# State-space scans in a fused decoder kernel: from 128 channels times one state to 8 channels times 16 states on the partitions

## The chip, the cores and the metric

The kernel runs on one core of a Trainium2 chip, in fp32 throughout the part that is discussed. The metric is the device time of one execution in microseconds. A core has five engines with instruction queues of their own: TensorE (PE, with its weight loads as PEld), VectorE (DVE), ScalarE (ACT), GpSimd (POOL) and SyncE (SP), which here issues all the DMAs.

## The reference, cut to what matters

A decoder of four layers runs on 4 sequences of 256 tokens with 256 features. Each layer has an attention part, a second mixing part and a feed-forward part; every part ends with a residual sum and a layer norm. In layers 0 and 1 the second mixing part is a state-space scan over the context `ctx_1024` (4 x 256 x 128), gated by the stream `x`, with 256 inner channels and 16 states per channel:

```python
x = einsum('ed,bld->bel', in_proj_w, hidden_states)      # 256 channels
u = silu(depthwise causal conv of 4 taps over x + conv_b)
x_dbl = einsum('ke,bel->bkl', x_proj_w, u)               # 8 + 16 + 16 rows
dt_lo, Bm, Cm = x_dbl[:, :8], x_dbl[:, 8:24], x_dbl[:, 24:]
delta = softplus(einsum('er,brl->bel', dt_proj_w, dt_lo) + dt_proj_b)
A = -exp(A_log)                                          # 256 x 16
def step(state, (d_t, B_t, C_t, u_t)):                   # state: b x 256 x 16
    state = state * exp(d_t[..., None] * A) + (d_t * u_t)[..., None] * B_t[:, None, :]
    return state, einsum('ben,bn->be', state, C_t)
y = (outputs of the steps + D * u) * silu(z)             # z is the stream x
```

Only the gate needs `x`. The scan itself depends on the context alone, so it can run beside other work.

## The kernel before

Features or channels lie on the 128 partitions in two chunks (DC = 2); a row of a tile runs over tokens. The program is written with the Tile framework: pools hand out buffers, semaphores are derived from the tiles' use, and the framework's scheduler puts the instructions of each engine into a fixed order when the program is built. On the chip every engine takes its queue in that order.

The class `Scans` holds both state-space passes. `begin(pre)` starts the generator `_steps` and `beside(n)` moves it on by n steps, so that the attention code can place scan steps between its own. `upto(b)` moves it on until sequence b is done, and `gate_pair` then gates that sequence, turns it back and adds it to the stream.

Pass one (`l0x`) runs beside the multi-query attention `run_mqa`: 32 pieces, n = 0 to 31, eight per sequence, each of four heads by 128 rows. A piece has scores, maxima (`nm`) and exponentials, transposes, sums (`o`) and an output product into the bank `acc`; the projections of query pairs (`queries`, with the rotation on DVE: `ropet`, `qT`) run four pieces ahead. In each piece the loop calls `K.scans.beside(2)`, and `gate_pair` is called for sequences 0, 1 and 2 at n = 10, 18 and 26 and for sequence 3 after the loop.

Pass two (`l1x`) is begun inside `run_thought`, a chain of four dependent iterations on 4 tokens followed by a gating of the whole stream; that function ends with `K.scans.beside(24)`. The rest runs beside the grouped attention `run_gqa`, one generator step per tile and then one per attention step. Its `gate_pair` calls are due after each sequence's attention.

Within `_steps` (lines 443 to 532) a prologue makes `u` (the convolution is folded into four matmuls with `taps`), writes the B and C rows to DRAM (`bcd`), and makes `delta` and `du = delta * u`, which stay in SBUF with 128 channels on the partitions. Then one generator step handles one state n of one sequence b for both chunks, 2 x 256 columns per partition:

- a DMA brings the B and C row of this state, spread over all partitions (`bc`, 256 KB);
- ACT makes two exponentials of 255 columns into `dA`, whose first column stays zero, so that the scan starts afresh at each chunk;
- DVE multiplies (`s = du * B`), scans over 512 columns (line 521) and multiplies by C;
- two steps later PE adds `s` to a PSUM bank by a product with the 128x128 identity (`ssmps`, fp32). After 16 states DVE adds the skip term and writes the result into `u`.

That makes 64 generator steps per pass, 16 for each sequence. `wk` gives four buffers for `bc` and for `s`, `dA` has three, and there is one PSUM bank.

Of the kernel before, what the change touches and what calls it, by code (L numbers as in the profile page):

```python
# [19 lines left out]
F32 = mybir.dt.float32  # L20
# [5 lines left out]
AF = mybir.ActivationFunctionType  # L26
# [4 lines left out]
ADD, SUB, MUL, MAX, MIN = ALU.add, ALU.subtract, ALU.mult, ALU.max, ALU.min  # L31

P = 128
B, L, D = 4, 256, 256
NT = B * L // P
DC = D // P
# [170 lines left out]
def again(ap, n):  # L207

    return ap.unsqueeze(1).to_broadcast([ap.shape[0], n, ap.shape[1]])
# [23 lines left out]
def run_mqa(K, w, more):  # L233
    nc, tc = K.nc, K.tc
    with ExitStack() as ctx:
        one = ctx.enter_context(tc.tile_pool(name="mqa1", bufs=1))
        wk = ctx.enter_context(tc.tile_pool(name="mqa2", bufs=2))
# [119 lines left out]
        N = 8 * B  # L357
# [3 lines left out]
        y = K.scans.y  # L361
# [6 lines left out]
        for n in range(N):  # L368
            shares(n)
            if n + 1 < N:  # L370
                scores(n + 1)
            if n + 4 < N:
                queries(n + 4)
            if n in (2, 3, 4, 5):
                rest.pop(0)()
            if n == 6:
                ready = ready_thought(K, more()) if K.fused(0) else iter(())
            if n > 9:
                next(ready, None)
            K.scans.beside(2)  # L380
            turn(n)
            if n:
                output(n - 1)
            sums(n)
            if n % 8 == 2 and n > 8 and K.fused(0):
                gate_pair(K, wk, y, n // 8 - 1)
        output(N - 1)
        if K.fused(0):
            gate_pair(K, wk, y, B - 1)
# [3 lines left out]

SSM_COLS = 19


class Scans:
    def __init__(self, K, ctx):  # L400
        tc = K.tc
        self.K = K
        self.one = ctx.enter_context(tc.tile_pool(name="ssm1", bufs=1))
        self.wk = ctx.enter_context(tc.tile_pool(name="ssm2", bufs=4))
        self.ps = ctx.enter_context(tc.tile_pool(name="ssmp", bufs=1, space=PSUM))
        self.dram = ctx.enter_context(tc.tile_pool(name="ssmd", bufs=2, space=bass.MemoryType.DRAM))

        self.dA = [self.one.tile([P, DC, L], F32, name=f"dA{k}") for k in range(3)]
        for t in self.dA:
            K.nc.gpsimd.memset(t[:, :, 0:1], 0.0)  # L410
        self.w = {}
        self.left = iter(())
        self.done = 0

    def load(self, pre):
        K = self.K
        self.w[pre] = {
            "in": K.load(self.one, f"{pre}_in", [P, D]),
            "xp": K.load(self.one, f"{pre}_xp", [P, DC, 40], "(c p) n -> p c n", p=P),
            "dt": K.load(self.one, f"{pre}_dt", [8, D]),  # L420
            "cols": K.load(self.one, f"{pre}_cols", [P, DC, SSM_COLS], "(c p) n -> p c n", p=P),
        }

    def bank(self):
        return self.ps.tile([P, 512], F32, name="ssmps", tag="ps")

    def begin(self, pre):

# [12 lines left out]
            next(self.left, None)  # L441

    def _steps(self, pre):
        K, nc, w, wk = self.K, self.K.nc, self.w[pre], self.wk
        cols = w["cols"]
        N = B * L
        u = self.one.tile([P, DC, N], F32, name="u", bufs=2)
        delta = self.one.tile([P, DC, N], F32, name="delta")
        du = self.one.tile([P, DC, N], F32, name="du")


        taps = []
        for j in range(4):
            t = wk.tile([P, D], F32, name="tap", tag="bc", padded_shape=[P, 2 * L])
            nc.sync.dma_start(out=t, in_=K.A[f"{pre}_cw"][:, j * D : (j + 1) * D].to_broadcast([P, D]))
            K.ptt(t, t, w["in"], MUL)
            taps.append(t)
        for h in range(2):
            for c in range(DC):
                ps = self.bank()  # L460
                for j in range(4):
                    K.mm(ps, taps[j][:, c * P : (c + 1) * P], K.ctxp[:, 2 * h : 2 * h + 2, j : j + L], j == 0, j == 3)
                K.act(u[:, c, 512 * h : 512 * h + 512], ps, AF.Identity, bias=cols[:, c, 0:1])
        K.act(u, u, AF.Silu)
        negA = self.one.tile([P, DC, 16], F32, name="negA")
        K.act(negA, cols[:, :, 2:18], AF.Exp)
        K.ts(negA, negA, -1.0, None, MUL)
        bc = self.dram.tile([2, 16, N], F32, name="bcd")
        for h in range(2):
            s = slice(512 * h, 512 * h + 512)  # L470
            xd = wk.tile([P, 512], F32, name="xd", tag="s")
            ps = self.bank()
            for c in range(DC):
                K.mm(ps[0:40, :], w["xp"][:, c, :], u[:, c, s], c == 0, c == DC - 1)
            nc.scalar.copy(xd[0:40, :], ps[0:40, :])
            for k in range(2):
                nc.sync.dma_start(out=bc[k, :, s], in_=xd[8 + 16 * k : 24 + 16 * k, :])
            for c in range(DC):
                ps = self.bank()
                K.mm(ps, w["dt"][:, c * P : (c + 1) * P], xd[0:8, :])  # L480

                K.ts(delta[:, c, s], ps, cols[:, c, 1:2], None, ADD)
                K.act(du[:, c, s], ps, AF.Abs, bias=cols[:, c, 1:2])
        K.act(du, du, AF.Exp, scale=-1.0)
        K.act(du, du, AF.Ln, bias=K.eps[1.0])
        for c in range(DC):
            K.stt(delta[:, c, :], delta[:, c, :], 0.0, du[:, c, :], MAX, ADD)
            K.tt(du[:, c, :], delta[:, c, :], u[:, c, :], MUL)

        turn = 0  # L490
        self.y = u

        late = []
        bank = {}

        def add(b, n, s):
            if n == 0:
                bank[b] = self.bank()
            y = bank[b]
            K.mm(y, K.ident, s.rearrange("p c l -> p (c l)"), n == 0, n == 15)  # L500
            if n == 15:
                for c in range(DC):
                    v = u[:, c, b * L : (b + 1) * L]
                    K.stt(v, v, cols[:, c, 18:19], y[:, c * L : (c + 1) * L], MUL, ADD)
                self.done += 1

        for b in range(B):
            lo = b * L
            for n in range(16):
                yield  # L510
                if len(late) > 1:
                    add(*late.pop(0))
                t = wk.tile([P, 2, L], F32, name="bc", tag="bc")
                nc.sync.dma_start(out=t, in_=bc[:, n, lo : lo + L].unsqueeze(0).to_broadcast([P, 2, L]))
                dA = self.dA[turn % 3]
                turn += 1
                for c in range(DC):
                    K.act(dA[:, c, 1:L], delta[:, c, lo + 1 : lo + L], AF.Exp, scale=negA[:, c, n : n + 1])
                s = wk.tile([P, DC, L], F32, name="s")
                K.tt(s, du[:, :, lo : lo + L], again(t[:, 0, :], DC), MUL)  # L520
                nc.vector.tensor_tensor_scan(  # L521
                    out=s.rearrange("p c l -> p (c l)"),
                    data0=dA.rearrange("p c l -> p (c l)"),
                    data1=s.rearrange("p c l -> p (c l)"),
                    initial=0.0,
                    op0=MUL,
                    op1=ADD,
                )
                K.tt(s, s, again(t[:, 1, :], DC), MUL)
                late.append((b, n, s))  # L530
        for t in late:
            add(*t)


def gate_pair(K, pool, y, b):

    K.scans.upto(b)
    gate = pool.tile([P, DC, L], F32, name="gate")

    K.act(gate, K.x[:, 2 * b : 2 * b + 2, :], AF.Silu)  # L540
    K.ptt(gate, gate, y[:, :, b * L : (b + 1) * L], MUL)
    for t in range(2):
        ps = K.tp.tile([P, 512], F32, name="ps", tag="tp")
        for c in range(DC):
            K.nc.tensor.transpose(ps[:, c * P : (c + 1) * P], gate[:, c, t * P : (t + 1) * P], K.ident)
        K.add_out(2 * b + t, ps[:, 0:D])
# [1782 lines left out]
def _layout(v):  # L2329
# [7 lines left out]

    a["l0a_wq"], a["l0a_wkv"], a["l0a_wout"] = v["L0_attn_Wq"], v["L0_attn_Wkv"], v["L0_attn_Wout"]
    a["l0a_rope"] = _rope_halves()

    for pre, s in (("L0_xattn_", "l0x_"), ("L1_xattn_", "l1x_")):
        g = lambda n, pre=pre: v[pre + n]
        a[s + "in"], a[s + "xp"], a[s + "dt"] = g("in_proj_w").T, g("x_proj_w").T, g("dt_proj_w").T
        a[s + "cw"] = g("conv_w").reshape(D, 4).T.reshape(1, 4 * D)
        a[s + "cols"] = np.concatenate(
            [g("conv_b")[:, None], g("dt_proj_b")[:, None], g("A_log"), g("D")[:, None]], 1
        )

    f = "L0_ffn_"
    for n in ("agg", "d1", "d2", "bc", "gate"):  # L2350
# [106 lines left out]
```

## Time and profile before

| | |
|---|---|
| time, median of 3 runs | 2405.0 us (2401.42 to 2425.04) |
| the profiled execution's own time | 2413.25 us |
| its span in the profile | 2411.4 us |
| busy PE, PEld | 2225.9 us (92%), 1514.3 us (63%) |
| busy DVE, ACT, POOL | 1461.5 us (61%), 788.5 us (33%), 259.7 us (11%) |
| mean granted TensorE clock | 0.948 of full speed |
| bytes moved by DMA | 139.50 MB |
| reads of the B and C rows (`bc<-bcd`) | 128 DMAs of 256.0 KB, 4.6 us from issue to landing |
| scans, line 521 | 128 of 128x512, 1214 ns each |
| first and last scan of pass one, of pass two | 87.7 and 354.7 us; 423.4 and 711.8 us |

Busy times are unions over an engine's instructions. A duration in a list of groups is that of one instruction from start to end; neighbours on one engine overlap somewhat, so the pitch on the timeline is shorter. "<-" after an idle time names what ended it. A released engine tells only of its own wait: idle time of an engine that isn't needed costs nothing.

### The profile page before, as it was taken

The page shows a single profiled execution, that of the slowest core. Times are in us where ns is not written, and L with a number is a line of the kernel's source. Part 1 is how long each engine was busy: PE and PEld are TensorE (multiplying, and loading weights), DVE is VectorE, ACT ScalarE, POOL GpSimd, SP SyncE. Part 2 cuts the span into 40 slices and gives each one's busy share as a digit, 9 for nine tenths or more (in the row PEclk, how much of TensorE's full clock was granted, in tenths as well). Part 3 has the DMA queues.
Part 4 walks back from the last instruction along what each step waited for, and adds up shares of the span by engine and source line. Part 5 has one row for each costly group of instructions (what it writes and reads, how often), then busy time and mean ns, then how long its engine had stood idle before and what let it go on. Part 6 is the DMA issues. An engine that isn't in the chain of part 4 may idle for free. (4 is left out here: it accounts for less than half of the span.)

```text
span 2411.4 us, 28602 instructions
## 1 busy us (share of the span) xinstructions
PE 2225.9 (92%) x10504; PEld 1514.3 (63%) x10504; DVE 1461.5 (61%) x3178; ACT 788.5 (33%) x1763; POOL 259.7 (11%) x419
## 2 busy tenths in 40 slices
PE   7889998589996999899999999999999988899998
PEld 4466664235434655546888888888876545477676
DVE  4899983898975211290355454444555668686366
ACT  4667674333441111162111111111112233243443
POOL 0000011220010322200001100011110001300001
PEclk9999999687986999999999999999997898999999
DMA  6222221232213544220132111120200011100000
GB/s 204 63 60 59 58 53 37 49 81 50 50 34 103 168 128 128 86 77 14 46 100 84 64 46 47 50 71 32 65 1 22 1 59 60 42 1 1 1 1 18
DMA packets 133747, 139.50 MB, mean 58 GB/s; under 512 B 13892, under 2 KB 121766, under 8 KB 131944
## 3 DMA queue, kind: packets, MB, share of 16 engines
q1 hardware_dynamic: 133608, 137.68, 19.9%
q8 instruction: 83, 1.36, 0.2%
q14 instruction: 56, 0.46, 0.1%
HBM read 134.79 MB, written 2.85 MB: 57 GB/s over the span
## 5 line engine op out<-in xcount | busy, mean ns | idle before, releaser
L133 PE MATMUL ps<-xw,xcT 128*128 128x256 f32 (+1 forms) x2304 | 518.9, 382 | 0.3 <-ACT YT L127 0.3
L133 PEld LDWEIGHTS ps<-xw,xcT 128*128 128x128 f32 x2304 | 430.8, 190 | 64.0 <-issue 1.9
L112 DVE TENSOR_TENSOR xp<-ps,xb 128x256 f32<-128x256 f32 x96 | 40.4, 421 | 229.5 <-PE ps L133 229.4
L133 PE MATMUL sc<-kT,qT 32*128 32x256 f32 (+2 forms) x768 | 168.1, 413 | 10.3 <-DVE qn L130 9.7
L133 PE MATMUL ssmps<-s,idz 128*128 128x512 f32 x256 | 147.9, 688 | 23.3 <-DVE s L112 22.4
L127 ACT ACTIVATE dA<-delta,negA 128x255 f32<-128x255 f32 x256 | 118.1, 501 | 136.2 <-DVE s L521 134.7
L521 DVE TENSOR_TENSOR_SCAN s<-dA,s 128x512 f32<-128x512 f32 x128 | 154.0, 1214 | 2.6
L133 PEld LDWEIGHTS sc<-kT,qT 32*128 32x128 f32 (+1 forms) x768 | 106.6, 204 | 74.1 <-issue 44.2
L112 DVE TENSOR_TENSOR hT<-u,a 128x512 f32<-128x512 f32 x48 | 33.1, 691 | 186.3 <-PE u L133 186.3
L127 ACT ACTIVATE sq<-xp 128x1024 f32<-128x1024 f32 x24 | 25.4, 1057 | 314.4 <-DVE xp L112 314.3
L170 POOL TENSOR_SCALAR rstd<-mv 128x2 f32<-128x2 f32 x48 | 11.6, 243 | 944.4 <-DVE mv L162 925.3
L130 DVE TENSOR_REDUCE qn<-sc 128x2 f32<-128x480 f32 (+1 forms) x192 | 87.0, 504 | 40.5 <-PE sc L133 39.6
L127 ACT ACTIVATE e<-sT 128x512 f32<-128x512 f32 x128 | 70.9, 590 | 108.1 <-PE sT L133 106.0
L133 PE MATMUL sT<-q,kT 32*128 32x256 f32 (+1 forms) x384 | 102.1, 506 | 3.9 <-ACT e L127 3.7
L1489 DVE TENSOR_TENSOR_SCAN dec<-xT,idz 128x256 f32<-128x256 f32 (+1 forms) x192 | 89.7, 535 | 22.1 <-DMA xT<-ad 22.1
L127 ACT ACTIVATE a<-g 128x512 f32<-128x512 f32 x48 | 28.7, 599 | 206.7 <-PE g L133 206.7
L133 PEld LDWEIGHTS ssmps<-s,idz 128*128 128x128 f32 x256 | 47.6, 209 | 75.0 <-DVE s L112 42.7
L133 PE MATMUL g<-xT,wj 128*128 128x512 f32 x192 | 92.1, 603 | 0.7 <-ACT rows L101 0.7
L133 PE MATMUL u<-xT,wj 128*128 128x512 f32 x192 | 91.2, 597 | 0.0
L133 PEld LDWEIGHTS y<-wj,hT 128*128 128x128 f32 x384 | 72.9, 190 | 26.6 <-issue 18.2
L133 PE MATMUL ps<-xT,wi 128*128 128x512 f32 x192 | 85.9, 604 | 3.9 <-ACT xin L127 3.9
L112 DVE TENSOR_TENSOR s<-du,bc 128x512 f32<-128x512 f32 x128 | 87.3, 691 | 3.4 <-PE ssmps L133 3.2
(504 smaller groups left out, 4087.8 us busy)
## 6 DMA issues: line engine op xcount, KB each, us to landing
bc<-bcd SPq DMA_DIRECT2D x128, 256.0 KB, 4.6
xw<-in_l2a_xw_dram SPq DMA_DIRECT2D x24, 768.0 KB, 4.9
xT<-ad SPq DMA_DIRECT2D x12, 1024.0 KB, 4.7
wj<-in_l1f_gate_dram SPq DMA_DIRECT2D x48, 128.0 KB, 2.7
wj<-in_l1f_up_dram SPq DMA_DIRECT2D x48, 128.0 KB, 3.1
wj<-in_l1f_down_dram SPq DMA_DIRECT2D x48, 128.0 KB, 3.1
sel<-cwd SPq DMA_DIRECT2D x32, 192.0 KB, 3.1
sel<-cwd SPq DMA_DIRECT2D x32, 128.0 KB, 3.5
```

The source lines that it names most:

```text
L112: self.nc.vector.tensor_tensor(out=out, in0=a, in1=b, op=op)
L127: self.nc.scalar.activation(out, in_, func, **kw)
L130: self.nc.vector.tensor_reduce(out=out, in_=in_, axis=AX.X, op=op, **kw)
L133: self.nc.tensor.matmul(out, lhsT=lhsT, rhs=rhs, start=start, stop=stop)
L170: self.nc.gpsimd.tensor_scalar(out=out, in0=in_, scalar1=add, scalar2=None, op0=ADD)
L521: nc.vector.tensor_tensor_scan(out=s.rearrange("p c l -> p (c l)"), data0=dA.rearrange("p c l -> p (c l)"), data1=s.rearrange("p c l -> p ...
L1489: nc.vector.tensor_tensor_scan(out=dec[:, k, h, :], data0=ap[:, h, at(bb, k, j) : at(bb, k, 2)], data1=K.idz[:, 0 : (2 - j) * P], initial=0.0,
```

## The change

The scan's layout is turned. A partition now holds one of 8 channels times one of 16 states, and a step takes two groups of 8 channels (g = 0, 1) and two sequences: 2 x 512 columns per partition. A pass has two halves (of two sequences each), two chunks c and eight steps k, 32 steps in all. Each step passes two yields, so that there are still 64 of them.

- `delta` and `du` are no longer read in place: both are written to DRAM (`ddd`, two writes of 1 MB), and each step reads back 8 channels, each spread over 16 partitions, by four DMAs of 256 KB on SP.
- The B and C rows are read once per half into `bct` (16 DMAs of 16 rows), in place of 32 reads of 256 KB.
- ACT makes two exponentials of 2 x 255 columns per step, DVE one multiply, one scan and one multiply over 1024 columns.
- The sum over the 16 states becomes two products per step with a 128x32 pattern `ssm_pick`, which writes a band of 32 PSUM partitions; four steps make a band.
- Pools: one ring `piece` of four buffers of 8 KB per partition takes the place of `bc`, `s`, `delta`, `du`, the taps and `xd`; `dA` has two buffers of 1024 columns.
- Pacing: `run_mqa` moves the generator by 2 and 3 steps in turn, and gates sequences 0, 1 and 2 at n = 17, 19 and 27. The input layout gains `ssm_pick` and an `A_log` in the new order.

```diff
-            K.scans.beside(2)
+            K.scans.beside(2 + n % 2)
...
-            if n % 8 == 2 and n > 8 and K.fused(0):
-                gate_pair(K, wk, y, n // 8 - 1)
+            if n in (17, 19, 27) and K.fused(0):
+                gate_pair(K, wk, y, (17, 19, 27).index(n))
...
-        self.dA = [self.one.tile([P, DC, L], F32, name=f"dA{k}") for k in range(3)]
+        self.dA = [self.one.tile([P, 2, 2, L], F32, name=f"dA{k}") for k in range(2)]
...
+        self.pick = K.load(self.one, "ssm_pick", [P, 4, 32], "p (k n) -> p k n", k=4)
...
+    def piece(self, shape):
+        n = int(np.prod(shape))
+        t = self.wk.tile([P, 4 * 512], F32, name="piece", tag="piece")[:, 0:n]
...
+        dd = self.dram.tile([D, 2, N], F32, name="ddd")
+        pair = [self.piece((2, N)) for _ in range(DC)]
+        xd = self.piece((2, 512))
...
         for c in range(DC):
-            K.stt(delta[:, c, :], delta[:, c, :], 0.0, du[:, c, :], MAX, ADD)
-            K.tt(du[:, c, :], delta[:, c, :], u[:, c, :], MUL)
+            K.act(pair[c][:, 1, :], pair[c][:, 1, :], AF.Exp, scale=-1.0)
+        for c in range(DC):
+            K.act(pair[c][:, 1, :], pair[c][:, 1, :], AF.Ln, bias=K.eps[1.0])
+        for c in range(DC):
+            delta, du = pair[c][:, 0, :], pair[c][:, 1, :]
+            K.stt(delta, delta, 0.0, du, MAX, ADD)
+            K.tt(du, delta, u[:, c, :], MUL)
+            nc.sync.dma_start(out=dd[c * P : (c + 1) * P], in_=pair[c])
...
-            K.mm(y, K.ident, s.rearrange("p c l -> p (c l)"), n == 0, n == 15)
+            for g in range(2):
+                band = 2 * (k // 4) + g
+                K.mm(y[32 * band : 32 * band + 32, :], self.pick[:, k % 4, :], s[:, g, :], k % 4 == 0, k % 4 == 3)
...
-        for b in range(B):
-            lo = b * L
-            for n in range(16):
-                yield
-                if len(late) > 1:
-                    add(*late.pop(0))
-                t = wk.tile([P, 2, L], F32, name="bc", tag="bc")
-                nc.sync.dma_start(out=t, in_=bc[:, n, lo : lo + L].unsqueeze(0).to_broadcast([P, 2, L]))
...
+        spread = lambda ap: ap.unsqueeze(1).to_broadcast([ap.shape[0], 16, ap.shape[1]])
+        for half in range(2):
+            at = slice(512 * half, 512 * half + 512)
+            bct = self.one.tile([P, 2, 512], F32, name="bct", bufs=2)
+            for k in range(2):
+                for g in range(8):
+                    nc.sync.dma_start(out=bct[16 * g : 16 * g + 16, k, :], in_=bc[k, :, at])
+            for c in range(DC):
+                for k in range(8):
+                    yield
...
+                    for j in range(2):
+                        for g in range(2):
+                            nc.sync.dma_start(out=t[:, j, g, :], in_=spread(dd[lo + 32 * g : lo + 32 * g + SG, j, at]))
...
+                    K.tt(s, s, again(bct[:, 0, :], 2), MUL)
+                    while late:
+                        add(*late.pop(0))
+                    if y is None:
+                        y = self.bank()
+                    yield
...
+                    nc.vector.tensor_tensor_scan(
...
+                    K.tt(s, s, again(bct[:, 1, :], 2), MUL)
+                    late.append((s, y, c, k, half))
```

## The prediction

> **What bounds the kernel now.** The change touches only the two state-space passes, so I looked first for where they lie, then at which engine is full there, then at the pitch of single instructions. The table by windows cuts the span at the first scan of pass one (beside the attention of layer 0), at its end, and in the same way for pass two (beside the thought block and the grouped attention). Columns: window, length, busy us of PE, PEld, DVE, ACT, POOL with counts, granted clock, DMA share, GB/s.
>
> ```profile
> core 0: us, PE busy (x) PEld busy (x) DVE busy (x) ACT busy (x) POOL busy (x), PEclk, DMA share, GB/s
> 0.00:33.00 33.00, 20.21 (x79) 14.54 (x80) 17.89 (x31) 8.29 (x27) 6.00 (x28) 0.95 0.97 319
> 105.00:358.00 253.00, 235.98 (x1056) 164.91 (x1055) 239.75 (x403) 178.38 (x511) 10.88 (x17) 0.99 0.27 59
> 417.00:450.00 33.00, 24.58 (x113) 10.65 (x114) 30.37 (x42) 23.21 (x41) 2.77 (x2) 0.68 0.33 74
> 450.00:507.00 57.00, 28.91 (x80) 14.78 (x80) 52.97 (x115) 12.69 (x28) 14.97 (x24) 0.75 0.24 55
> 507.00:728.00 221.00, 207.88 (x1124) 97.71 (x1123) 188.08 (x310) 83.64 (x170) 25.27 (x49) 0.85 0.22 47
> ```
>
> In pass one DVE is busy 239.75 of 253 us (95%) and PE 93%: two nearly full engines, DVE the fuller. In 417 to 507 DVE alone binds. In 507 to 728 it is the other way round: PE 94%, DVE 85%. So a change must be judged stage by stage.
>
> The timeline gives the pitch of the scans, which is shorter than the durations because neighbours overlap, and the end of pass one.
>
> ```profile
> 83.66 2.35 DVE L112 TENSOR_TENSOR du<-delta,u 128x1024 f32<-128x1024 f32 x2
> 86.53 1.28 DVE L112 TENSOR_TENSOR s<-du,bc 128x512 f32<-128x512 f32 x2
> 87.74 2.33 DVE L521 TENSOR_TENSOR_SCAN s<-dA,s 128x512 f32<-128x512 f32 x2
> 89.99 1.26 DVE L112 TENSOR_TENSOR s<-s,bc 128x512 f32<-128x512 f32 x2
> 91.17 1.28 DVE L112 TENSOR_TENSOR s<-du,bc 128x512 f32<-128x512 f32 x2
> ...
> 358.51 0.87 DVE L121 SCALAR_TENSOR_TENSOR u<-u,w_l0x_cols,ssmps 128x256 f32<-128x256 f32 x2 [1.83 <-PE ssmps L133]
> 365.49 0.76 DVE L112 TENSOR_TENSOR x<-acc,x 128x256 f32<-128x256 f32 x2 [6.11 <-PE acc L133]
> ```
>
> Two units (one state of one sequence) take 91.17 - 86.53 = 4.64 us. After the last scan only about 9 us pass until the attention's last sum (x<-acc): scans and attention end together. The groups give PE's prices; two instructions make one fp32 matmul.
>
> ```profile
> L133 PE MATMUL ssmps<-s,idz 128*128 128x512 f32 x128 | 62.8, 613 | 8.0 <-DVE s L112 8.0
> L133 PE MATMUL acc<-w_l0a_wout,oT 128*128 128x256 f32 x256 | 61.4, 380 | 0.0
> L133 PE MATMUL o<-pT,vt 128*128 128x512 f32 x96 | 48.7, 615 | 14.4 <-ACT pT L332 14.1
> L133 PE MATMUL ps<-w_d,hT 128*32 128x257 f32 x32 | 2.8, 388 | 0.5 <-ACT hT L739 0.5
> ```
>
> The last row is the nearest to the new sums: weights of 32 columns in neighbouring bands. 32 of them took 2.8 us, 0.09 us each, against 61.4/256 = 0.24 for the full width at about the same length, so bands overlap.
>
> **The DVE work of a step.** Before, two units hold 2 x 512 elements per partition: 4.64 us. After, one step holds 1024: two multiplies and one scan. The 1024-wide multiply has a pitch of 1.14 (85.93 - 83.66 for two). For the scan, its 512 form takes (89.99 - 87.74)/2 = 1.13, of which about 0.07 is fixed by the difference of the multiplies (0.60 and 1.14), so 2.2 for 1024. The sum is 4.48: 0.16 less per step, 5 us per pass of 32 steps. The elements stay the same and only the fixed parts go. It isn't the large saving that half as many instructions suggest. ACT loses 128 exponentials of 255 (59.4 us busy) for 64 of 510, nearest the 128x512 copy at 581 ns, so 37: some 22 us off an engine that is 71% busy in pass one and hidden behind DVE there.
>
> **The order, pass one.** The loop now takes 2.5 steps of the generator per attention piece instead of 2. The static order of DVE's instructions shows it: before, the first scan stands after 5 pieces' maxima and 8 query pairs, the last after 32 and 32. After, the first stands after 7 and 9, the last after 27 and 30. I make the sum from this.
> Start: delta and du go through DRAM. The exponential and logarithm are split by channel half, two more table loads at 1.28 us, so du is ready at 88.5 instead of 86.0. Then the read of four 256 KB pieces. The bc rows take 4.6 us to land and three more queue behind, about 7. First multiply at 97 instead of 86.5; bounds 92 (the read hidden but for 4 us) and 101 (both 1 MB writes have to land, 4.7 us in the nearest 1 MB row). SP issues in order, so the reads stand behind the second write, and that waits for DVE. The 16 loads of bct (some 0.36 us of SP each) are sent earlier and are hidden; without that cover they would cost 6 us.
> From first to last scan: 32 x 4.48 = 143, 21 query pairs at 2.71 (four operations on the timeline) = 57, 20 maxima at 1.04 = 21, ten norm rows at 1.2 = 12, four sums into u 2.5: 236 us. By the same prices the stretch before has 259 against 270 elapsed. At the same 96% I get 246, so the last scan's product is at 343 instead of 356.6.
> Tail: on PE, behind the last band product there now stand 28 acc matmuls (0.48 each, 13.4), 9 o (1.01, 9.1), 16 scores (6.5), 8 masks (2.2), 33 transposes (4.6) and 4 queries (2): 38 us. Before, 8 acc, 2 o and 8 transposes, 7 us. PE can't be quicker than its own work, and DVE idles there. Pass one: -13.6 + 31 = +17 us. What PE saves on the sums in the stretch before (62.8 halved) lies beside a full DVE and brings nothing.
>
> **DMA.** Per step 1.05 MB are read where two units read 0.52. In the first 33 us the 16 engines moved 319 GB/s at a share of 0.97; that is 3.3 us per step, the cheap end. A reading DMA lists 8 source rows 16 times; if only half the engines take part, 6.6 us, the dear end. Over the whole pass both hide under a step's 10 us. They don't where the order puts steps next to each other: the first 8 steps of pass one, at 4.48 each. There the cheap end costs nothing and the dear one adds 9 (the eighth piece lands at 95 + 7 x 6.6 = 141, its step ends at 146 instead of 137). In pass two (13 steps, with 27 us of thought work between) it adds 3. No row before has such a pattern at this size. The transfers of the burst are all led by 128 partitions, this one by 8, so I take the dear end and keep both.
> The Trainium skill speaks on this, in "DMA: Bandwidth & Descriptors", section "Why a DMA increments its semaphore by 16 and not by 1": a DMA uses the largest number of engines up to 16 that divides the slowest dimension of both patterns, here 8. By it the sum would be with the dear end; by the burst's row alone it would be 12 us lower. No run here shows it yet.
>
> **Pass two.** The same DRAM trip moves its first scan from 423 to about 435. The thought chain, spaced some 15 us per iteration by PE and ACT, doesn't wait; DVE has done 4 steps (8 units) when it ends instead of 14 units. The delay of 12 less 2 for the shorter steps, less 1 of thought work drawn ahead, is +9 where the grouped attention begins; +12 with the dear DMA. From 507 on PE binds. There 86 sum instructions take 56.3 us busy; in overlapping pairs half, so up to -28; DVE's 185 us at 96% set a floor at 193 of 221, the same 28. Nothing comes if DVE and its static order hold the pace, so 0 to -28; I take -14, since neither engine is free. Pass two: -2. One more load ahead of the first weights: +0.5.
>
> **Sum.** 17 + 9 + 12 - 14 + 0.5 = +25 us on this execution's 2413.25 us (span 2411.4, 1.9 around it). It stands 8 above the median of 2405.0, well inside the runs' spread, so I add the difference to the median: 2430. From the expert block on, the static order is the same as before.
>
> **Rivals.**
> *The cheap DMA*: everything as above, all 16 engines. For it: 319 GB/s in the burst. Against: the pattern. 2405 + 13 = 2418. Chance 0.30.
> *PE is the true bound in both passes* (the other side): it holds DVE up where DVE looks full, as 8.2 us before the last u of pass two show. Then pass one is freed of 31 us of sums against the tail's 31 and gains the earlier 14; pass two gains the full 28 less 9: -33, 2372. It decides from the point where the order's tail costs less than PE saves. Against: PE waited 8.0 us for DVE's s in pass one, DVE barely for PE. Chance 0.18.
> *The bands don't pay*: they don't overlap in pairs, or the granted clock, 0.85 in the last stage, falls towards the 0.70 it had from 560 to 590, because narrow products load the array less; 180 us at 0.70/0.85 are 218 again. No gain of 14: 2444. For it: clocks of 0.68 to 0.75 where PE is thin. Chance 0.17.
> The forecast has 0.35.
>
> **Numbers.** Low end: cheap DMA, the earliest start (-5) and the full 28, so -6, widened towards the PE rival to 2390; high end: dear, no gain and the late start, +43, 2450. A measurement of this kernel tells about 1% (24 us) from none. Slower by more: half and more of the forecast and nearly all of the third rival, 0.45. Faster by more: most of the second, 0.17. Within: 0.38.
>
> **What would show it.** The last scan of pass one near 345 to 352 and 30 us or more from there to x<-acc, PE full and DVE half idle between; first scans at 97 and 435; a scan of 128x1024 at 2.2 us pitch; band products at a quarter of a microsecond per instruction; piece reads spaced over 6 us among the first steps; 507 to 728 shortened by 14. It is wrong if x<-acc comes before 365, or if the second stage loses more than 20.

## The result: 4% slower, and the profile after

The changed kernel takes 2502.82 us (median of 4 runs, 2495.39 to 2514.74) against 2405.52 us before; the ratio is 1.039 with a 95% interval of 1.032 to 1.0465. The forecast of 2430 us, and the upper end of its range, 2450, were too low.

The profiled executions differ by 101.6 us of span (2513.0 - 2411.4). Four marks that both traces have cut this into stages: the copy of `tok` on DVE (pass one and its gates are over), the first maxima `qn` (the grouped attention begins in earnest), the first product of the expert block's router `lg` (pass two and its gates are over), and the end.

| us | before | after | difference | forecast |
|---|---|---|---|---|
| start to `tok` | 379.0 | 396.2 | +17.2 | +26 (17, and 9 for the transfers) |
| `tok` to first maxima `qn` | 142.4 | 165.2 | +22.8 | +12 |
| first maxima to router | 206.3 | 264.0 | **+57.7** | **-14** |
| router to end | 1683.7 | 1687.6 | +3.9 | 0 |

So one term is wrong by 72 us, and the errors of the others (-9, +11 and +4) nearly cancel, which is luck and not accuracy. The windows of after show it by stage: the scans of pass one, its tail, the stretch before the first scan of pass two, the stretch from the maxima to the router (columns as in the prediction).

```profile
core 0: us, PE busy (x) PEld busy (x) DVE busy (x) ACT busy (x) POOL busy (x), PEclk, DMA share, GB/s
98.40:340.40 242.00, 198.38 (x883) 121.38 (x884) 230.84 (x283) 142.07 (x376) 14.60 (x16) 0.94 0.40 136
340.40:381.60 41.20, 39.87 (x188) 28.18 (x186) 18.19 (x37) 27.60 (x82) 2.20 (x3) 1.00 0.00 0
396.20:458.10 61.90, 51.65 (x226) 25.75 (x224) 16.56 (x37) 29.47 (x38) 3.81 (x5) 0.69 0.22 74
561.40:825.40 264.00, 218.69 (x1081) 98.11 (x1081) 166.18 (x216) 73.09 (x122) 14.53 (x31) 0.71 0.20 66
```

In the last row no engine is full: PE 83%, DVE 63%, ACT 28%, DMA 20%. Before, PE was at 194.54 of 206.30 us there. Where every engine has gaps and no transfer is dense, a loop of waits is the first thing to look for. The timeline shows one turn of it (start, duration, instruction, idle time before it and what ended it):

```profile
643.62 1.07 PE L133 MATMUL ssmps<-piece,w_ssm_pick 128*32 128x512 f32 x2
...
645.65 2.41 SPq L535 DMA_DIRECT2D piece<-ddd  x4
...
649.19 0.72 ACT L127 ACTIVATE dA<-piece,negA 128x510 f32<-128x510 f32 x1 [5.71 <-DMA piece<-ddd]
...
653.75 0.72 ACT L127 ACTIVATE dA<-piece,negA 128x510 f32<-128x510 f32 x1 [3.84 <-DMA piece<-ddd]
654.37 1.06 ACT L127 ACTIVATE e<-sT 128x512 f32<-128x512 f32 x2
...
655.00 2.56 PE L133 MATMUL sT<-q,kT 32*128 32x512 f32 x4 [4.08 <-ACT e L127]
...
656.59 1.23 DVE L112 TENSOR_TENSOR piece<-piece,bct 128x1024 f32<-128x1024 f32 x1 [8.71 <-DMA piece<-ddd]
```

The band product of step 19 ends and frees its buffer; only then does SP send the four reads of step 23. They land over 11 us. Meanwhile ACT stands at the exponentials `dA` of step 23, with the attention's `e` queued behind them; PE waits for `e` before it can go on with `sT`; DVE stands at the step's multiply with the attention's maxima behind it. When all of this has moved on, the next band product comes, some 17 us after the last. The sums of the waits in that stretch say the same (us in total, times, longest):

```profile
SPq L535 <- PE ssmps L133: 160.2, 15, 17.1
```

```profile
ACT dA L127 <- DMA piece<-ddd: 76.6, 20, 9.8
```

Four buffers should allow three steps of reading ahead. Why there is none is in the static order, which is not a view of the profile. In PE's queue the band product of step k stands where the program wrote it, but the scheduler moved `dA` of step k+4 forward to just behind the point where its buffer comes free:

```
pass two, step              19  20  21  22  23  24  25
PE: band product after sT   14  18  22  26  30  34  38   (of 64)
ACT: dA after e              2   6   6  10  14  18  22   (of 64)
```

`dA` of step 23 stands after 14 exponentials, the product that frees its buffer after 14 `sT`: the same place. The order has a distance of zero between the release and the use, and the chip puts the issue and landing of 1 MB in between.

Before, `bc` and `s` were separate tiles: DVE freed the read buffer, so the sums on PE could lag without holding any transfer. The kernel before has this row among SP's waits in the same stretch, and none for PE's sums:

```profile
SPq L514 <- DVE s L112: 139.5, 28, 8.4
```

The change scans in the buffer that was read into, and so hands its release to PE.

Pass one went nearly as forecast: its first multiply is at 97.12 us, the last scan at 340.36, then DVE idles until PE has caught up.

```profile
97.12 1.23 DVE L112 TENSOR_TENSOR piece<-piece,bct 128x1024 f32<-128x1024 f32 x1 [3.76 <-DMA piece<-ddd]
98.45 2.29 DVE L552 TENSOR_TENSOR_SCAN piece<-dA,piece 128x1024 f32<-128x1024 f32 x1
...
340.36 2.28 DVE L552 TENSOR_TENSOR_SCAN piece<-dA,piece 128x1024 f32<-128x1024 f32 x1
...
345.61 0.75 DVE L121 SCALAR_TENSOR_TENSOR u<-u,w_l0x_cols,ssmps 128x512 f32<-128x512 f32 x1 [0.58 <-PE ssmps L133]
...
381.64 0.75 DVE L112 TENSOR_TENSOR x<-acc,x 128x256 f32<-128x256 f32 x2 [8.88 <-PE acc L133]
```

### The profile page after: what moved, and what is told of

Same layout as the page of the kernel before. It is cut to its first block, busy times and chain, and to the rows that moved or that the text cites. A ratio compares the mean times of both kernels' runs of the same rounds, so it can differ in the third digit from the quotient of the medians.

```text
span 2513.0 us, 28650 instructions
## 1 busy us (share of the span) xinstructions
PE 2252.3 (90%) x10504; PEld 1500.3 (60%) x10504; DVE 1448.4 (58%) x2978; ACT 768.3 (31%) x1643; POOL 262.7 (10%) x418
## 3 DMA queue, kind: packets, MB, share of 16 engines
q1 hardware_dynamic: 136664, 177.60, 21.7%
## 5 line engine op out<-in xcount | busy, mean ns | idle before, releaser
L133 PE MATMUL sc<-kT,qT 32*128 32x256 f32 (+2 forms) x768 | 186.5, 445 | 29.7 <-DVE qn L130 24.6
L112 DVE TENSOR_TENSOR piece<-piece,bct 128x1024 f32<-128x1024 f32 x128 | 155.8, 1237 | 78.4 <-DMA piece<-ddd 76.2
L133 PEld LDWEIGHTS sc<-kT,qT 32*128 32x128 f32 (+1 forms) x768 | 113.7, 219 | 97.9 <-issue 48.1
L133 PE MATMUL ssmps<-piece,w_ssm_pick 128*32 128x512 f32 x256 | 95.0, 791 | 61.7 <-DVE piece L112 57.4
L127 ACT ACTIVATE dA<-piece,negA 128x510 f32<-128x510 f32 x128 | 89.9, 718 | 191.5 <-DMA piece<-ddd 111.0
L552 DVE TENSOR_TENSOR_SCAN piece<-dA,piece 128x1024 f32<-128x1024 f32 x64 | 145.9, 2283 | 0.9
L133 PE MATMUL sT<-q,kT 32*128 32x256 f32 (+1 forms) x384 | 113.0, 544 | 19.1 <-ACT e L127 18.8
L127 ACT ACTIVATE e<-sT 128x512 f32<-128x512 f32 x128 | 70.9, 593 | 146.8 <-PE sT L133 146.2
L133 PE MATMUL y<-wj,hT 128*128 128x256 f32 x384 | 89.2, 379 | 0.0
```

Source lines behind the costliest of these rows:

```text
L112: self.nc.vector.tensor_tensor(out=out, in0=a, in1=b, op=op)
L127: self.nc.scalar.activation(out, in_, func, **kw)
L133: self.nc.tensor.matmul(out, lhsT=lhsT, rhs=rhs, start=start, stop=stop)
L552: nc.vector.tensor_tensor_scan(out=flat, data0=dA.rearrange("p g b l -> p (g b l)"), data1=flat, initial=0.0, op0=MUL, op1=ADD,)
```

## The experiments

Three theories stood against each other for the lost stage. *Loop*: what was just read off. *Slow read*: 1 MB per step on half the engines is too much. *Clock*: products of 32 columns lower the granted clock. The table has all runs; stages from each profile (us), the granted clock in the stretch from the first `qn` to the router, and the ratio to the kernel before with its interval.

| run | to `tok` | to first `qn` | `qn` to router | clock there | ratio |
|---|---|---|---|---|---|
| before | 379.0 | 142.4 | 206.3 | 0.84 | 1 |
| changed | 396.2 | 165.2 | 264.0 | 0.71 | 1.039 (1.032 to 1.0465) |
| e1 program order | 396.9 | 154.8 | 209.7 | 0.79 | 1.0176 (1.011 to 1.024) |
| e2 lead of 16 | 389.9 | 148.0 | 231.8 | 0.74 | 1.0179 (1.011 to 1.025) |
| e3 three buffers | 402.5 | 165.1 | 272.7 | 0.69 | 1.0401 (1.033 to 1.047) |
| e4 two rings | 395.3 | 149.2 | 236.4 | 0.74 | 1.0221 (1.015 to 1.029) |
| e5 = e1 + e2 | 387.3 | 148.7 | 212.3 | 0.75 | 1.011 (1.004 to 1.018) |
| e6 = e5 + pacing 2.25 | 382.8 | 146.2 | 214.7 | 0.77 | 1.0057 (1.0025 to 1.009) |
| e7 = e5 + 128 columns | 403.0 | 148.9 | 215.6 | 0.83 | 1.0203 (1.013 to 1.028) |
| e8 = e6 + e4 | 378.8 | 145.6 | 214.1 | 0.75 | 1.008 (1.004 to 1.012) |
| e9 before, sums left out | 378.6 | 143.0 | 207.9 | 0.71 | 0.9991 (0.997 to 1.002) |
| e10 = e8, half the sums | 380.1 | 146.5 | 214.4 | 0.73 | 1.0093 (1.006 to 1.013) |
| e11 = e8 + spare products | 381.3 | 144.3 | 219.4 | 0.77 | 1.0129 (1.006 to 1.020) |
| e12 = e8, pacing 2.125 | 371.8 | 155.6 | 214.0 | 0.75 | 1.0068 (1.003 to 1.011) |

Behind each row of stages stands one profile, and single executions differ. From the router on, PE's instructions come in the same order in before, changed, e2 and e9, yet that part took 1683.7, 1687.6, 1692.6 and 1681.3 us. From `tok` to the first scan of pass two, changed and e1 have the same order on PE and ACT, and took 61.9 and 52.9 us. So a few us in the table are no reading by themselves; the 54 and 32 us of e1 and e2 are far beyond this.

**e1: the order alone.**

```diff
+        def pin(ins):
+            if pre == "l1x" and turn > 12:
+                K.tc.keep_in_program_order(ins)
-                        K.act(dA[...], t[:, 0, g, :]..., AF.Exp, scale=negA[:, q : q + 1])
+                        pin(nc.scalar.activation(dA[...], t[:, 0, g, :]..., AF.Exp, scale=negA[:, q : q + 1]))
-                    K.tt(s, s, again(bct[:, 0, :], 2), MUL)
+                    pin(nc.vector.tensor_tensor(out=s, in0=s, in1=again(bct[:, 0, :], 2), op=MUL))
```

> Same bytes, reads, buffers and products; from step 13 of pass two on, a step's exponentials of dA and its first multiply are held in program order on ACT and DVE, so that they stand behind the exponentials e and the maxima that were written before them, and not right behind the band product that freed the buffer four steps earlier. Theory 'loop' (a step's read waits for the band product of four steps before; the exponentials dA and the multiply of that step were moved up to right behind it, so that every step pays issue and landing, about 11 us, on ACT and DVE, and with them PE's scores): from the first maxima qn to the router's first product 264 us become 195 to 215, and the time 2435 to 2455. Theory 'slow read' (1 MB on 8 engines is too much for a step's time): this stretch stays above 245, time above 2480. Theory 'clock' (products of 32 columns load the array less and the granted clock falls): stays above 240, with a clock below 0.8 there.

Measured: 264.0 became 209.7 us, as *loop* said; *slow read* and *clock* had it stay above 245 and 240. `dA` of step 23 now stands after 26 exponentials instead of 14. SP still waits for buffers in this stretch, 64.7 us for PE and 73.6 for DVE, but the waits now lie some 30 us ahead of the use: step 23's reads go out at 623.83 and its multiply runs at 656.42. ACT's waits for reads, 76.6 us in the changed kernel, are gone from its list. The window, to set beside the last row of the four above:

```profile
551.70:761.40 209.70, 189.71 (x1075) 86.09 (x1075) 168.05 (x210) 72.23 (x123) 13.84 (x28) 0.79 0.26 84
```

The median is 2459.93 us, 5 above what was expected, beside 2415.09 for the kernel before in the same comparison.

**e2: the lead of the reads.**

```diff
-        spread = lambda ap: ap.unsqueeze(1).to_broadcast([ap.shape[0], 16, ap.shape[1]])
+        spread = lambda ap: ap.unsqueeze(0).to_broadcast([16, ap.shape[0], ap.shape[1]])
-                for g in range(8):
-                    nc.sync.dma_start(out=bct[16 * g : 16 * g + 16, k, :], in_=bc[k, :, at])
+                nc.sync.dma_start(out=bct[:, k, :], in_=bc[k, :, at].unsqueeze(1).to_broadcast([16, SG, 512]))
```

with `ssm_pick` and `alog` laid out to match.

> Partitions as 16 states times 8 channels instead of 8 channels times 16 states, so that every read of a piece and of bct is led by 16 rows; the same bytes, buffers and order. All theories: if the lead sets how many engines move a transfer, reads back to back run at a DMA share near 1 and not 0.53, and the first 8 steps of pass one come at 4.5 us each and not 5.2. 'Slow read': the stretch from the first maxima to the router falls from 264 to below 215. 'Loop': the landing shortens from about 11 to 6 or 7 us and the loop stays, so some 4 us for each of the ten slow steps: 215 to 230. 'Clock': no change of this stretch, 255 or more. Pass one ends 3 to 8 us earlier. Time by 'loop' 2440 to 2465.

Busy share of the DMA engines in 40 slices of 100 to 112 us, in tenths, in the changed kernel and then in e2, with reads back to back:

```profile
DMA  5545555555455555555575555455455545545545
DMA packets 1258, 2.44 MB, mean 203 GB/s; under 512 B 73, under 2 KB 73, under 8 KB 1257
```

```profile
DMA  4899778999999989999999999799999998642000
DMA packets 1637, 2.98 MB, mean 249 GB/s; under 512 B 191, under 2 KB 191, under 8 KB 1635
```

Led by 8 rows the reads hold half the engines and 203 GB/s, steadily; led by 16 they fill nearly all, and then the queue runs empty. This is what the Trainium skill says in "DMA: Bandwidth & Descriptors", section "Why a DMA increments its semaphore by 16 and not by 1", of the largest number up to 16 that divides both slowest dimensions. Scans 3 to 6 come 4.45 us apart (109.03 to 122.39) instead of 5.2 (109.73 to 125.35), and `tok` is 6.3 us earlier. In the slow stretch the loop stays, but its turn is shorter:

```profile
644.82 1.92 PE L133 MATMUL ssmps<-piece,w_ssm_pick 128*32 128x512 f32 x4
...
646.85 2.44 SPq L534 DMA_DIRECT2D piece<-ddd  x4
...
653.65 1.23 DVE L112 TENSOR_TENSOR piece<-piece,bct 128x1024 f32<-128x1024 f32 x1 [2.75 <-DMA piece<-ddd]
```

From issue to the multiply 6.8 us instead of 10.9, and the stretch 231.8, just above the 215 to 230 of *loop*; *slow read* wanted less than 215, *clock* 255 or more.

**e3: three buffers.**

```diff
-        self.wk = ctx.enter_context(tc.tile_pool(name="ssm2", bufs=4))
+        self.wk = ctx.enter_context(tc.tile_pool(name="ssm2", bufs=3))
```

> Three buffers for a step's piece instead of four. 'Loop': the stretch from the first maxima to the router stays within 15 us of 264, since the exponentials stand right behind the product that frees the buffer in either order; what is lost is in pass one and beside the thought block, where reads ahead hid the landing, 10 to 40 us. If it is plainly the number of buffers (too few for the read's time), the stretch itself becomes longer by 40 us or more. 'Clock': stretch unchanged, all else too.

The stretch became 272.7, 9 us more: within the 15 of *loop*, far from the 40 of a plain shortage of buffers. A loop that has no distance to begin with loses little by one buffer less. Elsewhere it lost 16 us against e1, which up to there differs from the changed kernel in nearly nothing (5.6 to `tok`, 10.3 from there to the maxima), and 10 to 40 were expected. Against the changed kernel's own profile it is 6.3 to `tok` and nothing from there to the maxima, where that execution was slow itself (see e4). The whole time is no clear loss: 1.0401 beside 1.039.

**e4: two rings in the same space.**

```diff
-        t = self.wk.tile([P, 4 * 512], F32, name="piece", tag="piece")[:, 0:n]
+        t = self.wk.tile([P, 2 * 512], F32, name="pdu" if k else "pdt", tag="pdu" if k else "pdt", bufs=5 if k else 3)[:, 0:n]
...
-            nc.sync.dma_start(out=dd[c * P : (c + 1) * P], in_=pair[c])
+            for k in range(2):
+                nc.sync.dma_start(out=dd[c * P : (c + 1) * P, k], in_=pair[c][k])
```

> In the same 32 KB, two rings: three buffers of 4 KB for the delta half, which the exponentials free on ACT, and five for the half that is scanned in place, which the band product frees on PE; delta and du are written to DRAM in four transfers. 'Loop': ACT's exponentials no longer wait for PE, DVE's multiply still does, so the stretch from the first maxima to the router falls from 264 to 225 to 250. Plain number of buffers: below 225. 'Slow read' and 'clock': unchanged, above 250. First scans of both passes 0 to 4 us earlier, since half a transfer lands sooner.

236.4, within *loop*'s 225 to 250; *slow read* and *clock* wanted more than 250. The first scan of pass two comes 48.0 us after `tok` instead of 61.9. Part of that is not the edit: e1, whose held order begins only later, has 52.9, at a clock of 0.81 where the profiled execution of the changed kernel had 0.69. So about 9 of the 22.8 us lost in that stage belong to that one execution and not to the order. The clock is part of it at most, since e3, with the same order, has 54.2 us at a clock of 0.71. What is left for the smaller transfers is 5 of the 14 us, less than single executions differ there.

**e5: order and lead together.**

> The program order of pinned and the 16-row lead together. 'Loop': with the loop gone the landing no longer counts beside the grouped attention, so the lead adds there nothing (first maxima to router 203 to 212, as 209.7 with the order alone) and only its gains elsewhere come on top: 6 us in pass one, 4 to 7 beside the thought block; time 2440 to 2450 against the same before. 'Slow read': both gains of that stretch add up, below 195.

212.3, no less than with the order alone: once the loop is gone, the landing costs nothing there. That the two gains don't add, 54 and 32 alone and 52 together, is the best single sign of the loop; *slow read* had the two gains add up, to below 195. Outside the stretch the lead keeps its gains against e1: 9.6 us to `tok`, 6.1 from there to the maxima.

**e6: the pacing.**

```diff
-            K.scans.beside(2 + n % 2)
+            K.scans.beside(2 + (n % 4 == 3))
...
-            if n in (17, 19, 27) and K.fused(0):
+            if n in (17, 19, 29) and K.fused(0):
```

> As the one with both, and the attention of layer 0 draws 2.25 instead of 2.5 half steps per piece, with the third output gate moved from piece 27 to 29. Theory of the tail (PE's work behind the last band product, with DVE idle, is what pass one lost): the last scan comes 8 to 14 us later, the last sum x<-acc 6 to 14 us earlier, time 6 to 14 us below the one with both. Rival (DVE and PE each full, the tail costs nothing): x<-acc within 3 us.

The last scan moved from 331.5 to 343.3 us, `x<-acc` from 372.7 to 368.2: 4.5 us, where 6 to 14 were expected and the rival had 3. The profiled spans differ by 8.3 us, the medians by 15 (2445.15 and 2430.18), more than this stage explains. So the tail costs time, but less than its length.

**e7: full width.** The products go into the whole bank; a window of 128 columns over a zero-padded matrix puts the 8 channels in place.

```diff
-                band = 2 * (k // 4) + g
-                K.mm(y[32 * band : 32 * band + 32, :], self.pick[:, k % 4, :], s[:, g, :], k % 4 == 0, k % 4 == 3)
+                lo = 64 * (k // 4) + 32 * g + SG * (k % 4)
+                K.mm(y, self.pick[:, 120 - lo : 248 - lo], s[:, g, :], k + g == 0, k + g == 8)
```

> As the one with both, and each sum over states as a product of 128 columns (8 channels in their place, zeros elsewhere) into the whole bank, instead of 32 columns into a band: the same number of products, no two beside each other. Theory 'bands save PE time': PE's busy time from the first maxima to the router rises by 10 to 25 us and the stretch by half of that or more; pass one ends 5 to 15 us later. Theory 'clock' (narrow products lower the granted clock): the clock of that stretch rises by 0.03 or more and the stretch gets no longer.

Both were half right. Pass one ends 15.7 us later, so the bands are worth their width there. In the grouped attention the sums take 53.3 us of PE instead of 32.9, yet PE's busy time is 2.7 us *less* (197.02 in e5) and the stretch only 3.3 longer, at a clock of 0.83 instead of 0.75:

```profile
551.90:767.50 215.60, 194.28 (x1080) 93.45 (x1080) 169.71 (x211) 72.24 (x124) 14.57 (x29) 0.83 0.27 78
```

So wide products did go with a higher clock, as *clock* had it, and the higher clock brought no time.

**e9, e10, e11: what a sum costs there.** That called for the plainest price: take the sums away from the kernel before.

```diff
+            if pre == "l0x" or n in (0, 15):
-            K.mm(y, K.ident, s.rearrange("p c l -> p (c l)"), n == 0, n == 15)
+                K.mm(y, K.ident, s.rearrange("p c l -> p (c l)"), n == 0, n == 15)
```

> The kernel before, with 14 of 16 sums over states left out in pass two (in each sequence only the first and the last state are added). It prices what the sums cost there. Theory 'PE holds the stage' (the forecast's term of 14, bounds 0 to 28): from the first maxima to the router 206 us become 180 to 196. Rival 'clock gives it back' (the full-width sums are what keeps the granted clock at 0.84): the clock falls to 0.75 to 0.79 and the stretch stays above 200.

The rival holds, with a clock still lower than it named. The groups of PE by shape, 521 to 728 us of before and 521 to 729 us of e9 (count, then busy us and mean ns):

```profile
L133 PE MATMUL sc<-kT,qT 32*128 32x256 f32 x248 | 57.7, 453 | 2.6 <-DVE qn L130 2.6
L133 PE MATMUL sT<-q,kT 32*128 32x512 f32 x128 | 51.1, 692 | 2.8 <-ACT e L127 2.8
L133 PE MATMUL ssmps<-s,idz 128*128 128x512 f32 x76 | 49.5, 743 | 1.1 <-DVE s L112 1.0
L133 PE MATMUL o<-e,ones 128*32 128x256 f32 x256 | 21.5, 446 | 0.0
```

```profile
L133 PE MATMUL sc<-kT,qT 32*128 32x256 f32 x250 | 68.2, 546 | 8.7 <-DVE qn L130 8.6
L133 PE MATMUL sT<-q,kT 32*128 32x512 f32 x128 | 56.0, 764 | 4.8 <-ACT e L127 4.7
L133 PE MATMUL o<-e,ones 128*32 128x256 f32 x256 | 27.7, 554 | 0.7 <-ACT e L127 0.7
...
L133 PE MATMUL ssmps<-s,idz 128*128 128x512 f32 x10 | 6.7, 764 | 0.1
```

The sums fell from 49.5 to 6.7 us, and the same attention products that stayed became longer: 10.5, 4.9 and 6.2 us in these three groups. The stretch is 207.9 instead of 206.3, where the theory *PE holds the stage* had 180 to 196. Its windows, before and e9:

```profile
521.40:727.70 206.30, 194.54 (x1077) 91.73 (x1077) 173.38 (x278) 78.84 (x157) 18.01 (x37) 0.84 0.21 44
```

```profile
521.60:729.50 207.90, 186.19 (x1011) 91.45 (x1010) 169.06 (x277) 80.36 (x157) 18.32 (x35) 0.71 0.19 44
```

Of the 43 us of sums, then, PE's busy time fell by 8; some 34 went into longer products. PE's idle time grew from 11.8 to 21.7 us, most of it in waits for DVE's maxima `qn`, for ACT and for POOL. But e9 is not the removal alone: the scheduler also gave the rest a new order, in which 212 of DVE's 276 instructions in the stretch keep their sequence.

In e10, where 206 of DVE's 210 keep theirs, it is half of the band products that are left out:

```diff
-            for g in range(2):
+            for g in range(2 if pre == "l0x" or k % 4 in (0, 3) else 0):
```

> The kernel with all improvements, and in pass two half of the band products left out (the middle two of each four steps). 'PE holds the stage': first maxima to router 214 us become 200 to 207. 'Clock gives it back': within 4 us of 214 at a clock of 0.70 to 0.75.

214.4 against 214.1, at 0.73: the same answer. The sums fell from 31.9 to 17.3 us and PE's busy time from 197.25 to 189.34, so about half of what was taken away came back in longer products and half in waits. A rival is left here: a chain of waits through DVE, ACT and PE may hold this stage, and the clock only follow PE's lighter load. No run takes work from DVE or ACT there, so the two are not told apart. In e11 wide bf16 products with zero weights stand before and behind each step's band products:

```diff
+            wide = lambda a, b: K.mm(y.rearrange("p (a b) -> p a b", a=4), self.zerob, again(K.identb, 4), a, b)
+            if extra:
+                wide(k == 0, False)
             for g in range(2):
...
+            if extra:
+                wide(False, k == 7)
```

> The kernel with all improvements, and in pass two two more bf16 products of 128 columns by 512 per step, which add zeros to the same bank (some 8 us of PE's time in the stretch). 'Clock' as a matter of array width: clock up from 0.75 to 0.79 or more, the stretch falls from 214 to below 210. 'PE holds the stage' alone: the clock stays and the stretch becomes longer by 4 to 8 us. If the clock follows what the products really switch: no change of clock.

The spare products took 17.5 us of PE, not the 8 expected. The clock rose from 0.75 to 0.77, short of the 0.79 asked for, and the stretch became 5 us longer, as for *PE holds the stage*. Both are small against what single executions differ by, and the intervals of e11 and e8 overlap, so it is not shown that added work was paid for.

**e8 and e12: all that helped.** e8 is e6 with the two rings of e4.

> All that helped together: program order, 16-row lead, slower pacing and the two rings with transfers to DRAM by halves. Expected from the parts: pass one ends 10 to 20 us before the changed kernel, beside the thought block 12 to 18 us less, grouped attention 200 to 212; 2415 to 2440, that is not clearly faster than before, since the trip through DRAM at both starts stays.

Pass one now ends where it did before (378.8 against 379.0). The 10 us of span that are left over are 3 in the second stage and 8 in the third, which at 214.1 stays above the 200 to 212 expected. The time, 2433.88 us, is in the expected range, and the ratio is no lower than that of e6 without the rings. e12 changes the pacing once more:

```diff
-            K.scans.beside(2 + (n % 4 == 3))
+            K.scans.beside(2 + (n % 8 == 7))
...
-            if n in (17, 19, 29) and K.fused(0):
+            if n in (17, 19, 31) and K.fused(0):
```

> The kernel with all improvements, drawing 2.125 half steps per piece in pass one, third output gate at piece 31. Theory of the tail: last scan 4 to 8 us later, the last sum x<-acc 3 to 9 us earlier than 364 us, time 3 to 9 us lower, so level with the kernel before. Rival (the balance is reached; the gates now stand behind each other at the end): x<-acc earlier, but the copy of tok 0 to 6 us later.

The last scan came 2.3 us later than in e8 (4 to 8 expected), `x<-acc` at 358.3 instead of 364.2 and `tok` 7 us earlier; the following stage was 10 us longer, with 55.4 us instead of 47.5 to the first scan, at a clock of 0.72 instead of 0.83. So neither theory foresaw where the gain went, and the ratio doesn't differ clearly from e8's. No version found is faster than before: the nearest, e6, is 0.6% slower.

## Why the prediction was wrong, step by step

- **The step that failed** is "Over the whole pass both hide under a step's 10 us", and with it the third term of the sum, -14 for the grouped attention, measured +57.7. I compared the reading time of a step (3.3 or 6.6 us) with its pitch, as if reads were free to run ahead. I had counted buffers but not asked who frees them: with the scan in place it is the last reader, PE, which stands latest in the order. With a release-to-use distance of zero each turn paid the 10.9 us from issue to multiply. e1 restores the distance and gets 54 us back.
- **The -14 itself had no base.** I read "PE 94% busy" as time that comes back when PE's work falls. In e9 43 us of sums go and nothing comes back, nor in e10: the lower bound of 0 that stood beside the -14 was the right one. With the loop gone, the stage stands 3 to 8 us above before (e1, e5, e8), not 14 below. This is the outcome of the third rival, and its reason holds in part: the clock was higher with 128 columns (e7, 0.83) than with 32 (e5, 0.75). But e9 lowers it too by taking away full-width products, and e7's higher clock made the stage no shorter. Whether the clock or the waits for DVE and ACT hold the stage stays open.
- **Pass one** was right in its parts. Start 97 (97.12). The last scan's product was put at 343 (cheap) to 352 (dear) and came at 343.21, the cheap end. Tail 38 us of PE (345 to 381.64, 37). To `tok` the whole was +17.2 of +26.
- **The dear DMA** was half right: 8 of 16 engines fits the share of 5 tenths, but a step took 5.2 us, not 6.6. The estimate halved the burst's 319 GB/s; the reads made 203. The first steps lost the expected time (step 8 ended at 145.3 us, its last multiply at 144.1 plus 1.2; forecast 146), but by the last scan it was made up, so the 9 us of the dear DMA did not reach the end of pass one. DVE was busy for 95% of that stretch.
- **Pass two's start**, from `tok` to its first scan (44.4 us before), was put at +12 (423 to 435). It is +8.5 in e1 and +17.5 in the profiled execution of the changed kernel, with the same order.
- **The pairs of bands**: 76 instructions took 32.8 us where 76 full ones took 49.5, a third less, not half. The clocks were 0.71 and 0.84; busy time times clock is 23 and 42 us, near half. So the halving itself was nearly right, and the time it should have freed is what did not come back.

```profile
L133 PE MATMUL ssmps<-piece,w_ssm_pick 128*32 128x512 f32 x76 | 32.8, 928 | 2.1 <-DVE piece L112 2.1
```

- Of the signs named beforehand, the first start (97), the tail and the 2.2 us of a scan came true. The first scan of pass two came at 458.1, not 435 (17 of the 23 us are pass one's own delay), the reads among the first steps 5.2 us apart, not over 6, and a band instruction took 32.8/76 = 0.43 us, not a quarter. The last sign, the second stage losing more than 20, spoke against the forecast by either reading: 22.8 us from `tok` to the maxima, 57.7 from there to the router.

## What to carry to other kernels

When a buffer that a transfer fills is also worked on in place, ask which engine releases it and where that engine's release stands in the fixed order against the next use: count the distance in that order, not the buffers. A busy engine in a stretch with a clock below 1 need not be a store of time: price a removal by taking the work away, before building on it. And when two cures gain 54 and 32 us alone and 52 together, this points to one loop that both act on.

## What the runs showed of the hardware that was not expected

The granted clock gave back much of what PE saved, and waits the rest. Busy time times clock in the stretch from the maxima to the router is 163 us before (194.54 x 0.84), 148 in e5 (197.02 x 0.75), 132 in e9 (186.19 x 0.71); the stretch is 206, 212 and 208 us. The Trainium skill's "TensorE: Matmul & The Clock Gate", section "Part 1: The HAM clock gate", says that the clock is set by how busy PE has been of late. These three rows agree in direction (busy for 94, 93 and 90% of the stretch), e7 does not: 90% at a clock of 0.83. The same page's section "HAM oscillation — how this bites in real kernels" gives idle gaps of about 3.4 us as what costs the clock; the longest wait of PE in the stretch was 2.4 us in before and 2.3 in e5, at 0.84 and 0.75, so such gaps don't explain the difference between these two. The width of the products bears on it, by the one pair e5 and e7; what else sets the clock there is left open. So is this row of e12, behind the gate of pass one: PE full, and half the clock, though from 358 to 400 us no wait of PE was longer than 0.9 us.

```profile
380.00:390.00 10.00, 10.00 (x22) 3.85 (x25) 1.01 (x5) 0.58 (x1) 1.02 (x1) 0.50 0.16 49
```

That row lies in the stretch in which the 7 us won in e12's pass one went again. Why the clock fell there, and not in e8, was not tried.
